# A four-layer graph network on one core: chunks of messages are summed by accumulating transfers before the matrix W2, the last senders of all planes are found in one shared tile, there are fewer columns, and elu is summed on TensorE

## The chip, the cores and the metric

The kernel runs on one core of a Trainium2 chip. The metric is the device time of one execution in microseconds (us), lower is better. Engines are called as in the profile: PE is TensorE (PEld its weight loads), DVE is VectorE, ACT is ScalarE, POOL is GpSimd, SP is SyncE, which only issues transfers here.

## The reference, cut to what matters

There are 64 graphs ("batches") of 256 nodes with 128 features. Every layer adds its result to `x` and begins with a layer norm without weights and a relu, `h`.

```python
# layer 0: multi-head attention (8 heads of 16), masked by adj == 0, weighted by adj, normalised again
x = x + L0(h, adj)
# layer 1: attention from one sender score and one receiver score, masked softmax
x = x + L1(h, adj)
# layer 2: two graph attention (GAT) layers of 4 heads, each followed by elu(o) = max(o,0) + exp(min(o,0)) - 1
x = x + L2(h, adj)
# layer 3: a message for every pair (i, j), weighted by the adjacency
m_j, m_i = h @ W1[:D], h @ W1[D:]
pre = m_j[:, None, :, :] + m_i[:, :, None, :] + b1
msg = gelu(layernorm(pre, g1, be1))
agg = einsum('bijo,bij->bio', msg, adj)
x = x + layernorm(concat([h, agg]) @ W2 + b2, g2, be2)
```

The adjacency is sparse: each pair is an edge with probability of about 1/16 (3.1% made symmetric), and every node has an edge to itself. In layer 3 a message counts only where `adj` is not zero.

## The kernel before, in words

**Streams.** Each batch goes through six stages, each a Python generator that yields after every few instructions: `first` (f: loads, layer 0, the receivers' ranks), `second` (s: layer 1 and the first GAT), `third` (t: the second GAT, `x2`), `lists` (l: which senders each receiver of layer 3 has), `edges` (e: messages and their sums), `fourth` (u: the last norm and the output). In one round the six stages work on six different batches. The string `ORDER` says in which order the generators are advanced within a round: a letter runs its stage to the next yield. `START` gives the round in which a stage begins, and how many of its first letters are passed over, which shifts the stage within the round. Every engine and SP executes its instructions in exactly that order (`tc.manual_schedule()`), and an instruction that waits holds up all behind it on its engine.

**Ranks.** `mha` counts the zeros of each row of the adjacency on PE, and ranks the receivers by their number of senders (L380 to L401). Two indirect transfers on POOL (`in_order`, L695) write the adjacency rows to DRAM in the order of the ranks (`adr_d`), two more write the normalised features (`xn_d`).

**Lists.** `lists` needs three numbers for every edge: the sender's number (`key`), the edge weight and the variance of its message. They are packed into three `planes` of [128, 2, 256], each element carrying the sender's key in its upper bits. MAX8 (L824) finds the eight largest of a row, MATCH_REPLACE8 (L827) takes them out, and so on until `MAXES` = 40 for the block of the 128 highest ranks and 24 for the other are in `best`. The bits are sorted out again (L808 to L851), and the result goes to DRAM as `code_d` (sender numbers, fp16) and `ws_d` (weights and 1/std).

**Edges.** A slot s holds the s-th sender of every receiver. `GROUPS` says how many of the ranked receivers can have a sender in a slot: slots 0 to 15 have all 256 columns, later slots fewer. The groups are laid into five chunks of 1,024 columns: four full ones of four slots, and a last one with the rest. For each chunk `load_chunk` broadcasts code, 1/std and weight to all partitions (`cb`, `rb`, `wb`, L885), with two buffers of each. DVE compares the code with the sender numbers (`chosen`, L903); ACT writes the receivers' part into PSUM (`seeded`, L913); PE adds the senders' part by multiplying with that one-hot matrix (`gather`, L367); DVE multiplies by 1/std (L953), ACT applies gelu (L955), POOL multiplies by the weight (L957). `aggregate` then sums over slots by multiplying each slot with `w2b` on PE into the one tile `agg` (L363); from slot `SUMMED` on, DVE sums the slots of a group first (L929). The chunk before is aggregated while the present one is made.

**elu.** `gat` makes `o` (L661), POOL takes the minimum with 0 (L665), ACT the exponential (L667), POOL max(o, 0) - 1 (L669), and DVE adds the two (L671). The first GAT's result is transposed on PE (L348) and copied by ACT to `g1T`; the second's is added to `xt` (L732).

**Overflow.** Two tests find a receiver with more senders than slots or group hold (L840, L868, L870). If one did, the kernel `every_pair` would run after this one and do all pairs.

Of the kernel before, what the change touches and what calls it, by code (L numbers as in the profile page):

```python
# [8 lines left out]
F32 = mybir.dt.float32  # L9
# [20 lines left out]
SLOTS, MAXES = 36, (40, 24)  # L30
GROUPS = [(0, 4, 256), (4, 4, 256), (8, 4, 256), (12, 4, 256),
          (16, 1, 176), (17, 2, 168), (19, 3, 84), (22, 4, 36), (26, 2, 14), (28, 8, 11)]
SUMMED = 19
# [5 lines left out]
    "fffffstleeeelettfflssfteftesltflseftlfeselfettesetfstststseflfeflletsfetfseeefftfsfllfslffltsessusuf"  # L39
    "uustfffffefffffufutfffletfusfefstetlfsfltltffutettftsulstsfsslefeteleefelflefseetullllslsllesltelllt"  # L40
    "llllllllllelsftsttlfetftllllefsstflusllfltlusfsettffssulleefsefefefeffeetefeleleeeesfefseslslseeeeee"
    "eeelletseelessesfslffselselusslfselffllslstltfleelllfsfllslsllftelsuslfeltslllllefssfllselusseefltss"
    "sesueelleeeeeeelteelsssle"
)

START = {"f": (0, 0), "s": (1, 0), "t": (2, 0), "l": (3, 0), "e": (4, 0), "u": (5, 10)}
# [6 lines left out]
def listed_pairs(  # L53
# [223 lines left out]
    V.tensor_tensor(g1_c, g1_c, down_c, op=ALU.mult)  # L277

# [17 lines left out]
    best = ct([P, 3, NB, MAXES[0]], "best")  # L296
    V.memset(best, 0.0)
    beyond = ct([SLOTS, N], "beyond")
    cap_t, cap_v = ct([SLOTS, 1], "cap_t"), work.tile([1, SLOTS], F32, tag="cap_v", name="cap_v")
    for slot, n, cap in GROUPS:  # L300
        V.memset(cap_v[:, slot:slot + n], cap)
    nc.sync.dma_start(cap_t, cap_v)
    V.tensor_scalar(beyond, nums[:SLOTS, :N], cap_t, None, op0=ALU.is_ge)
    over, over_t = ct([P, 1], "over"), ct([SLOTS, N], "over_t")
    V.memset(over, 0.0)
    V.memset(over_t, 0.0)
# [69 lines left out]
    def mha(hT, ad, adT, xt, rank, adr_d, st):  # L376
# [3 lines left out]
        V.tensor_scalar(mask, ad, 0.0, None, op0=ALU.is_equal)  # L380
# [11 lines left out]
        yield  # L392
        zs = wt([P, N + NB], "zs", st)
# [9 lines left out]
        for nb in range(NB):  # L403
            in_order(adr_d, ad, rank, nb)
            yield
# [93 lines left out]
        for nb in range(NB):  # L499
            V.tensor_tensor(cx[:, nb].rearrange("p (h d) -> p h d", h=HEADS), pn[:, nb, :, 1:1 + HD],  # L500
                            z[:, nb, :, None].to_broadcast([P, HEADS, HD]), op=ALU.mult)
            yield
# [59 lines left out]
    def gat(hT, off, offT, weights, st):  # L562
# [16 lines left out]
        V.tensor_copy(h1, x1)  # L579
# [5 lines left out]
        V.tensor_scalar(ys, x1, rcv, snd, op0=ALU.mult, op1=ALU.add)  # L585
        yield
        V.tensor_scalar(yt[0], x1, snd, rcv, op0=ALU.mult, op1=ALU.add)
# [83 lines left out]
        V.tensor_tensor(o, o, ex, op=ALU.add)  # L671
        yield
        return o


    def several(shape, name, pool=const, dtype=F32, n=2):
# [3 lines left out]
                           several([P, NB, N], "ad"), several([P, NB, N], "adT"))  # L680
# [8 lines left out]
    adr_d, xn_d, ur_d = (several([N, N], "adr_d", dram, n=5), several([N, D], "xn_d", dram, n=3),  # L689
# [7 lines left out]
    def first(b):  # L697

        xt, ad, adT = x1_[b % 3], ad_[b % 2], adT_[b % 2]
# [12 lines left out]
        yield from mha(hT, ad, adT, xt, rank_[b % 6], adr_d[b % 5], "0")  # L712

    def second(b):

        xt, ad, adT = x1_[b % 3], ad_[b % 2], adT_[b % 2]
# [8 lines left out]
        yield from transposed(g1, g1T_[b % 2])  # L725

    def third(b):
# [4 lines left out]
        V.tensor_tensor(x2, xt, g2, op=ALU.add)  # L732
# [8 lines left out]
    def lists(b):  # L741
# [4 lines left out]
        adr, xr, hT = wt([P, NB, N], "adr", "4"), wt([P, NB, D], "xr", "4"), wt([P, N], "hT", "4")  # L746
# [26 lines left out]
        V.tensor_scalar(ciT, p[:, N:], b1_c, down2_c, op0=ALU.add, op1=ALU.mult)  # L773
# [47 lines left out]
        for n in range(3):  # L821
            for nb in range(NB):
                for r in range(0, MAXES[nb], 8):
                    V.max(best[:, n, nb, r:r + 8], planes[n][:, nb])  # L824
                    yield
                    if r + 8 < MAXES[nb]:
                        V.match_replace(planes[n][:, nb], best[:, n, nb, r:r + 8], planes[n][:, nb], 0.0)  # L827
                        yield
# [793 lines left out]
```

## Time and profile before

| | |
|---|---|
| median of 3 runs | 5219.54 us (5213.21 to 5232.44) |
| the profiled execution | 5207.46 us |
| its span | 5205.6 us |
| PE busy | 4491.0 us, 86% |
| DVE busy | 4538.1 us, 87% |
| ACT busy | 3334.4 us, 64% |
| POOL busy | 2672.9 us, 51% |
| DMA, hardware queue | 34.8% of 16 engines, 493.85 MB |
| DMA, software queue (POOL) | 1.9%, 33.58 MB |
| mean granted TensorE clock | 0.957 of full speed |

The span runs from the first to the last instruction; the execution's own time lies 1.9 us over it. In the tables of groups a row gives line, engine, operation, what is written and read, the count, then busy time in all and the mean of one in ns, then the idle time of the engine just before these instructions and who ended it. Busy time counts overlapping instructions once; the mean is of each one's own duration, so that busy over count is below the mean where instructions overlap, as matmuls do. A row of waits gives who waited for whom, the total in us, how often, and the longest.

### The profile page before, as it was taken

Reading aid. Unit: us, or ns where it says so; the run is one execution under the profiler, and the core shown is the slowest. Engines: PE = TensorE matmul, PEld = TensorE weight load, DVE = VectorE, ACT = ScalarE, POOL = GpSimd, SP = SyncE. Lnnn points to the kernel's source line nnn. Section 1 sums busy time; section 2 is a strip of 40 time slices with the busy share of each in tenths; the row PEclk is TensorE's granted clock in tenths of the full one; section 3 lists DMA queues with packets and bytes.
Section 4 is the critical chain, followed back from the end, with each engine's and each line's share of the span. In section 5 each row is a group of like instructions: output and inputs, shape, how many; then the busy total and the mean of one; then the engine's idle time right before and its main releaser. Section 6 shows DMA issues by size and latency. Waiting matters only on the chain. (4 is left out here: it accounts for less than half of the span.)

```text
span 5205.6 us, 89976 instructions
## 1 busy us (share of the span) xinstructions
PE 4491.0 (86%) x30294; PEld 2636.3 (51%) x30294; DVE 4538.1 (87%) x12551; ACT 3334.4 (64%) x6264; POOL 2672.9 (51%) x2890
## 2 busy tenths in 40 slices
PE   5888898888988988988988988988888988998974
PEld 3455555555555555555555555555555555555542
DVE  3688988989988988989988988988988988998985
ACT  2466666666666666667666666666666666666662
POOL 2345555555545545555545545545545545555543
PEclk9899999999999999999999999999999999999997
DMA  1033433333343343343343343343333343343344
GB/s 23 12 113 97 104 116 98 104 117 102 100 118 103 98 118 105 96 118 109 93 118 109 93 118 108 92 118 108 93 118 96 105 117 103 99 118 102 99 117 118
DMA packets 754582, 533.27 MB, mean 102 GB/s; under 512 B 490809, under 2 KB 647614, under 8 KB 754110
## 3 DMA queue, kind: packets, MB, share of 16 engines
q1 hardware_dynamic: 739774, 493.85, 34.8%
q0 software_dynamic: 14336, 33.58, 1.9%
q8 instruction: 241, 3.95, 0.3%
q14 instruction: 231, 1.89, 0.1%
HBM read 479.41 MB, written 47.84 MB: 101 GB/s over the span
## 5 line engine op out<-in xcount | busy, mean ns | idle before, releaser
L957 POOL TENSOR_TENSOR ms<-ms,wb 128x1024 f32<-128x1024 f32 x320 | 754.8, 2359 | 582.9 <-ACT ms L955 476.0
L367 PE MATMUL up<-oh,cj 128*128 128x512 f16 x2560 | 672.1, 400 | 172.0 <-DVE oh L903 96.6
L470 POOL TENSOR_TENSOR ew<-e,adT 128x512 f32<-128x512 f32 x512 | 668.7, 1328 | 62.0 <-ACT e L465 62.0
L363 PE MATMUL agg<-ms,w2b 128*128 128x256 f32 (+2 forms) x2432 | 674.9, 401 | 2.8 <-POOL ms L957 2.8
L824 DVE MAX8 best<-pl 128x8 f32<-128x256 f32 x1536 | 629.1, 420 | 27.0
L330 POOL TENSOR_SCALAR rs<-mv 128x2 f32<-128x2 f32 x256 | 57.5, 225 | 1098.0 <-DVE mv L323 1092.6
L955 ACT ACTIVATE ms<-ms,be,g 128x1024 f32<-128x1024 f32 x320 | 396.7, 1240 | 325.9 <-DVE ms L953 324.5
L629 ACT ACTIVATE ps<-ps 128x512 f32<-128x512 f32 x512 | 277.5, 589 | 414.3 <-PE ps L363 414.2
L367 PEld LDWEIGHTS <-cj 128*128 128x128 f16 x2560 | 251.9, 102 | 494.0 <-issue 162.3
L363 PEld LDWEIGHTS agg<-ms,w2b 128*128 128x128 f32 x2432 | 418.2, 197 | 158.9 <-issue 113.0
L903 DVE TENSOR_SCALAR oh<-cb,code 128x1024 f16<-128x1024 f16 x640 | 344.7, 580 | 163.0 <-DMA cb<-code_d 163.0
L953 DVE TENSOR_TENSOR ms<-up,rb 128x512 f32<-128x512 f32 x640 | 421.1, 682 | 62.9 <-PE up L367 25.8
L827 DVE MATCH_REPLACE8 pl<-best,pl 128x256 f32<-128x256 f32 x1152 | 470.6, 408 | 0.0
L913 ACT ACTIVATE up<-ci 128x512 f32<-128x512 f32 (+6 forms) x896 | 403.0, 477 | 20.7 <-DVE m L605 12.4
L465 ACT ACTIVATE e<-ps 128x512 f32<-128x512 f32 x512 | 276.5, 591 | 173.3 <-PE ps L363 173.3
L444 DVE TENSOR_REDUCE mx_p<-ps 128x2 f32<-128x512 f32 x512 | 332.5, 682 | 19.6 <-PE ps L363 17.4
L605 DVE TENSOR_REDUCE m<-ps 128x2 f32<-128x512 f32 x512 | 331.7, 679 | 6.8 <-PE ps L363 6.8
L638 ACT ACTIVATE y<-ps 128x512 f32<-128x512 f32 x512 | 283.0, 595 | 36.7 <-PE ps L367 33.1
L695 POOL DMA_INDIRECT adr_d<-ad,rank x128 | 134.1, 1048 | 316.8 <-DMA adr_d<-ad,rank 195.6
L340 ACT ACTIVATE xn<-x,nm,rs 128x128 f32<-128x128 f32 x512 | 235.8, 487 | 88.5 <-POOL nm L333 87.8
L363 PE MATMUL ps<-qT,kT 32*128 32x256 f32 x2048 | 291.8, 402 | 0.4 <-DVE qT L451 0.4
L363 PE MATMUL ps<-kT,qT 32*128 32x256 f32 x2048 | 289.9, 400 | 0.0
(295 smaller groups left out, 10615.1 us busy)
## 6 DMA issues: line engine op xcount, KB each, us to landing
rb<-ws_d SPq DMA_DIRECT2D x256, 512.0 KB
wb<-ws_d SPq DMA_DIRECT2D x256, 512.0 KB
cb<-code_d SPq DMA_DIRECT2D x256, 256.0 KB
ad<-in_adj_dram SPq DMA_DIRECT2D x64, 256.0 KB
adr<-adr_d SPq DMA_DIRECT2D x64, 256.0 KB
rb<-ws_d SPq DMA_DIRECT2D x64, 168.0 KB
wb<-ws_d SPq DMA_DIRECT2D x64, 168.0 KB
x<-in_x_dram SPq DMA_DIRECT2D x64, 128.0 KB
```

Of the source, the lines that this page charges most:

```text
L363: return T.matmul(o, lhsT=lhsT, rhs=rhs, start=start, stop=stop)
L367: return T.matmul(o, lhsT=lhsT, rhs=rhs, start=False, stop=False, skip_group_check=True)
L444: V.tensor_reduce(mx_p[:, nb, :, r + j, 0], ps[j], axis=AX.X, op=ALU.max)
L470: G.tensor_tensor(ew[:, r], e[:, r], adT[:, nb:nb + 1, :].to_broadcast([P, HG, N]), op=ALU.mult)
L605: V.tensor_reduce(m[:, k + j], ps[j], axis=AX.X, op=ALU.max)
L824: V.max(best[:, n, nb, r:r + 8], planes[n][:, nb])
L827: V.match_replace(planes[n][:, nb], best[:, n, nb, r:r + 8], planes[n][:, nb], 0.0)
L903: V.tensor_scalar(oh[:, jb], cb, code[:, jb:jb + 1], None, op0=ALU.is_equal)
L913: S.activation(ps[:, lo - h * 512:hi - h * 512].rearrange("p (k n) -> p k n", n=cap), ci_[u][:, None, :cap].to_broadcast([P, (hi - lo) // ...
L953: V.tensor_tensor(ms[:, hs], ps[h], rb[:, hs], op=ALU.mult)
L955: S.activation(ms, ms, AF.Gelu, bias=be1_c, scale=g1_c)
L957: G.tensor_tensor(ms, ms, wb, op=ALU.mult)
```

## The change

- In `edges`, POOL no longer hands every chunk to PE. The first chunk's messages stay in a tile of their own (`whole`), and the next three are added to it by accumulating transfers from POOL's queue. W2 is applied to this sum, four products, and to the last chunk. The step of aggregating the chunk before is gone.
- In `lists`, MAX8 and MATCH_REPLACE8 take 24 and 16 numbers from the rows of the two blocks. What is left of the first 16 rows of one block and the first 26 of the other, of all three planes, goes by six SP transfers into one tile `tail` of 126 rows; up to 16 more are found there, and six transfers bring them back into `best`.
- `GROUPS` has smaller capacities: the last chunk has 898 columns instead of 1,024, and one group more. Slot 19 is no longer summed with others on DVE.
- `gat` returns the two parts of elu. For `g1T` PE multiplies both with the identity and sums them in PSUM; for `x2` POOL adds one part to `xt` and DVE the other.
- Two scalings and a cast in `gat`, and `ciT` in `lists`, go from DVE to ACT. `cx` in `mha` is one operation instead of two.
- The number of zeros of each row goes along as a 257th column of the adjacency (`adz`, `adr_d`), and the overflow test compares its minimum with a table, once at the end.
- `ORDER` and `START` are written anew: 386 letters instead of 425, of them 83 e instead of 96 and 75 l instead of 99.

```diff
-SLOTS, MAXES = 36, (40, 24)
+SLOTS = 36
+MAIN, MORE, TAIL = (24, 16), 16, (16, 26)
 GROUPS = [(0, 4, 256), (4, 4, 256), (8, 4, 256), (12, 4, 256),
-          (16, 1, 176), (17, 2, 168), (19, 3, 84), (22, 4, 36), (26, 2, 14), (28, 8, 11)]
-SUMMED = 19
+          (16, 1, 154), (17, 2, 130), (19, 1, 98), (20, 2, 84), (22, 3, 40), (25, 3, 14), (28, 8, 7)]
+SUMMED = 20
...
-START = {"f": (0, 0), "s": (1, 0), "t": (2, 0), "l": (3, 0), "e": (4, 0), "u": (5, 10)}
+START = {"f": (0, 0), "s": (1, 3), "t": (2, 0), "l": (3, 3), "e": (4, 8), "u": (5, 9)}
...
+        V.tensor_copy(adz[:, :, N], p[:, N:N + NB])
+        yield
...
-        for nb in range(NB):
-            V.tensor_tensor(cx[:, nb].rearrange("p (h d) -> p h d", h=HEADS), pn[:, nb, :, 1:1 + HD],
-                            z[:, nb, :, None].to_broadcast([P, HEADS, HD]), op=ALU.mult)
-            yield
+        V.tensor_tensor(cx.rearrange("p b (h d) -> p b h d", h=HEADS), pn[:, :, :, 1:1 + HD],
+                        z[:, :, :, None].to_broadcast([P, NB, HEADS, HD]), op=ALU.mult)
         yield
...
-        V.tensor_copy(h1, x1)
+        S.activation(h1, x1, AF.Copy)
...
-        V.tensor_scalar(ys, x1, rcv, snd, op0=ALU.mult, op1=ALU.add)
-        yield
-        V.tensor_scalar(yt[0], x1, snd, rcv, op0=ALU.mult, op1=ALU.add)
+        S.activation(ys, x1, AF.Identity, scale=rcv, bias=snd)
+        yield
+        S.activation(yt[0], x1, AF.Identity, scale=snd, bias=rcv)
...
-        V.tensor_tensor(o, o, ex, op=ALU.add)
-        yield
-        return o
+        return o, ex
...
-        yield from transposed(g1, g1T_[b % 2])
+        p = pt()
+        for nb in range(NB):
+            for n in range(2):
+                mm(p[:, nb * P:(nb + 1) * P], g1[n][:, nb, :], ident, start=n == 0, stop=n == 1)
+        yield
+        S.activation(g1T_[b % 2], p[:, :N], AF.Copy)
+        yield
...
-        V.tensor_tensor(x2, xt, g2, op=ALU.add)
+        G.tensor_tensor(x2, xt, g2[0], op=ALU.add)
+        yield
+        V.tensor_tensor(x2, x2, g2[1], op=ALU.add)
...
-        V.tensor_scalar(ciT, p[:, N:], b1_c, down2_c, op0=ALU.add, op1=ALU.mult)
+        S.activation(ciT, p[:, N:], AF.Identity, scale=down2_c, bias=b1d_c)
...
+        V.tensor_tensor(fewest, fewest, adr[:, :, N], op=ALU.min)
+        adr = adr[:, :, :N]
...
+        tail, tops8 = wt([3 * sum(TAIL), N], "tail", "4"), wt([3 * sum(TAIL), MORE], "tops8", "4")
+        def part_of(n, nb):
+            at = n * sum(TAIL) + sum(TAIL[:nb])
+            return slice(at, at + TAIL[nb])
         for n in range(3):
             for nb in range(NB):
-                for r in range(0, MAXES[nb], 8):
+                for r in range(0, MAIN[nb], 8):
                     V.max(best[:, n, nb, r:r + 8], planes[n][:, nb])
                     yield
-                    if r + 8 < MAXES[nb]:
-                        V.match_replace(planes[n][:, nb], best[:, n, nb, r:r + 8], planes[n][:, nb], 0.0)
-                        yield
+                    V.match_replace(planes[n][:, nb], best[:, n, nb, r:r + 8], planes[n][:, nb], 0.0)
                     yield
+                nc.sync.dma_start(tail[part_of(n, nb)], planes[n][:TAIL[nb], nb])
+                yield
+        for r in range(0, MORE, 8):
+            V.max(tops8[:, r:r + 8], tail)
+            yield
+            if r + 8 < MORE:
+                V.match_replace(tail, tops8[:, r:r + 8], tail, 0.0)
+                yield
+        for n in range(3):
+            for nb in range(NB):
+                nc.sync.dma_start(best[:TAIL[nb], n, nb, MAIN[nb]:MAIN[nb] + MORE], tops8[part_of(n, nb)])
+                yield
...
-        V.tensor_tensor(over, over, best[:, 0, 0, SLOTS:SLOTS + 1], op=ALU.max)
-        yield
...
-        G.tensor_tensor(far, rows_t[:SLOTS], beyond, op=ALU.mult)
-        yield
-        G.tensor_tensor(over_t, over_t, far, op=ALU.add)
         yield
...
-            ms = edge.tile([P, COLS], F32, tag="ms", name="ms", bufs=3)
+            w = widths[c]
+            halves = [slice(0, 512), slice(512, w)]
+            ms = edge.tile([P, COLS], F32, tag="ms" if c else "whole", name="ms", bufs=3 if c else 1)
...
-            G.tensor_tensor(ms, ms, wb, op=ALU.mult)
+            G.tensor_tensor(ms[:, :w], ms[:, :w], wb[:, :w], op=ALU.mult)
             yield
+            if c == 0:
+                whole = ms
+            elif c < CHUNKS - 1:
+                G.dma_start(whole, ms, accum_op=ALU.add)
+                yield
...
             yield
-            if before is not None:
-                yield from aggregate(c - 1, before)
-            before = ms
+        yield from aggregate(0, whole)
         yield
-        yield from aggregate(CHUNKS - 1, before)
+        yield from aggregate(CHUNKS - 1, ms)
```

## The prediction

> **What bounds the kernel now.** I read the page's busy shares first, then a stretch of ten batches in the middle, then DVE's waits there, then the groups that the change touches.
>
> ```profile
> PE 4491.0 (86%) x30294; PEld 2636.3 (51%) x30294; DVE 4538.1 (87%) x12551; ACT 3334.4 (64%) x6264; POOL 2672.9 (51%) x2890
> L859 DVE CAST code<-pt x64: 415/417/418, 274.7 to 5136.8; 36x256 f16<-36x256 f32 x64
> 2000.00:2771.80 771.80, 685.50 (x4715) 404.31 (x4714) 701.80 (x1935) 519.58 (x972) 416.01 (x445) 0.98 0.39 106
> DVE oh L903 <- DMA cb<-code_d: 104.0, 41, 3.7
> DVE o L671 <- POOL o L669: 61.7, 40, 1.6
> DVE code L859 <- PE pt L855: 12.4, 40, 0.3
> ```
>
> Line 2 is an operation that runs once a batch: its first and last start give a **period** of (5136.8 - 274.7)/63 = 77.2 us, and a fixed part of 5205.6 - 63 x 77.2 = 343 us. Line 3 (columns: window, its length, busy of PE, PEld, DVE, ACT, POOL, clock, DMA share, GB/s) covers ten periods. Per period DVE is busy 70 us (69.7 over the 40 periods from 1046.5), PE 68.5, ACT 52, POOL 41.6. Two engines are at 90%, each in a hand-written order. DVE's idle 7.5 us is in the last three lines (40 periods): 2.6 us for the first chunk's code columns, 1.5 us for POOL inside elu, 0.3 us; the rest is gaps too small for the view. The page's chain of waits names only the tail of the run, each share 0%, and carries nothing. So a microsecond counts if it leaves both DVE and PE, or if it is a wait on their queues.
>
> ```profile
> L824 DVE MAX8 best<-pl 128x8 f32<-128x256 f32 x1536 | 629.1, 420 | 27.0
> L827 DVE MATCH_REPLACE8 pl<-best,pl 128x256 f32<-128x256 f32 x1152 | 470.6, 408 | 0.0
> L827 DVE MATCH_VALUE_LOAD pl<-best,pl 128x8 f32 x1152 | 103.7, 90 | 28.9
> L671 DVE TENSOR_TENSOR o<-o,ex 128x256 f32<-128x256 f32 x128 | 86.5, 676 | 101.6 <-POOL o L669 101.6
> L363 PE MATMUL agg<-ms,w2b 128*128 128x256 f32 x2048 | 606.8, 417 | 0.0
> L957 POOL TENSOR_TENSOR ms<-ms,wb 128x1024 f32<-128x1024 f32 x320 | 754.8, 2359 | 582.9 <-ACT ms L955 476.0
> POOL adr_d L695 <- DMA adr_d<-ad,rank: 195.6, 63, 4.3
> 2618.00:2620.00 2.00, 2.00 (x12) 1.16 (x11) 1.93 (x6) 1.04 (x4) 0.00 (x0) 1.00 1.06 420
> ```
>
> The matmul row is 32 records a batch for 16 full-width products with W2: each fp32 product is two records. They overlap, so its price is busy over count, 606.8/2048 = 0.296 us, not the mean 417 ns. The last line is DMA at its fullest: 420 GB/s.
>
> **What the Trainium skill says.** (1) "DMA: Bandwidth & Descriptors", section "Anatomy of one DMA — SWDGE (gpsimd) path": a transfer takes about 2.0 us plus bytes over 436 GB/s, most of the fixed part being the receipt. This trace agrees: 420 GB/s above, and POOL's indirect transfers land 2.2 to 2.4 us after issue. (2) "Collectives: The Full Stack", section "The bandwidth ceiling: the fold count and why AG ≠ RS ≠ AR": a reducing transfer is slow because it reads two sources, not because of the add. No run here shows one yet. (3) The first page, "Rules for kernel authors": an accumulate must wait for the earlier accumulate of the same bytes; the built order of the changed kernel has those waits on POOL. (4) "SBUF — State Buffer", section "Who interferes with whom": a DVE operation with two SBUF inputs and a POOL operation that reads SBUF block each other. The trace agrees: L671 takes 409 ns at best, 676 on average.
>
> **The change part by part, per batch.** From the two built orders, counts are exact.
>
> *Lists, DVE.* MAX8 24 to 15, MATCH_REPLACE8 18 to 15; on the shared tail two and one are added. -9 x 0.410 - 3 x (0.409 + 0.090) + 2 x 0.410 + 0.499 = **-3.9**. The overflow test (L840, 0.15) becomes a minimum of two columns (0.15) and a copy of two counts from PSUM (about 0.2, nearest the reciprocal of 128x8 from PSUM, 0.2): +0.2.
>
> *elu and gat, DVE.* Both o + ex go (L671): -2 x 0.676; third() keeps one add, with ex in place of o. The cast of h1 (0.286), ys (0.407) and yt (0.405) move to ACT, twice a batch: -2.2. ciT moves too (-0.54); cx is one operation for two (-0.14). Together **-4.2**. The last chunk is 898 columns for 1024: two comparisons (0.54 each), one product (0.66) and four sums shrink, **-0.4**. DVE in all -8.3: 69.7 becomes **61.4**.
>
> *PE.* Four full chunks are summed to one before W2: 12 of 16 products go, -24 x 0.296 = **-7.1**. g1T: two transposes (0.25 each) become four matmuls of 128x128 with the identity, eight records at the price of pt<-gs,lo (72.8/512 = 0.142): +0.6. Narrower gathers -4 x 0.2625 x 0.25 = -0.26; slot 19 gets its own product, +0.2. PE -6.5: 68.4 becomes **61.9**.
>
> *ACT* gains 2 x 0.38 + 4 x 0.59 + 0.47 + 0.2 for one more seeding, **+3.8**, to 55.5. Table loads stay eight a round. It is hidden as long as ACT, at 79% of the new period, is not late for PE.
>
> *POOL.* far and over_t go (-1.5), xt + o comes (+0.74), the last product is narrower (-0.3), and three accumulates are issued. An issue isn't in the trace; nearest is DMA_INDIRECT, 1.05 us; below, it can't be under zero; above I allow 2.5. 3 x 1.05: **+2.1** in all, to 43.1, with idle time to hide in.
>
> *The accumulates' landing* (T). Plain, 0.52 MB costs 2.0 + 1.2 = 3.2 us by the skill's formula; with two reads 2.0 + 2.5 = **4.5**, my estimate; at the mean 107 GB/s of the middle stretch two reads take 10, my upper end. Order on POOL: product 1, accumulate 1, both adr_d writes, product 2, accumulate 2 (waits for 1), both uu gathers, product 3, accumulate 3 (waits for 2). Cover of the first wait is two issues, the 3.1 us between them (195.6/64) and a product: 2.1 + 3.1 + 2.36 = 7.5 us. Cover of the second is 2.1 + 2.36 = 4.5. PE's first product with the sum stands behind the last chunk's gather, mask and score matmuls of mha and a whole y product, over 8 us later. At 4.5 us all is covered. DMA work grows from 0.39 x 77.2 = 30 us by 3 x 2.5, to half of the period.
>
> *SP.* Twelve tail transfers and three more chunk pieces are issued, 0.44 us each (median of the cb issues): 6.6 us, in front of the next x, ad, code_d and chunk loads. *New DVE waits:* the tail's last transfer needs 0.44 + 2.3, and DVE has four reductions, three small operations and ym in front of the MAX8 on tail, 2.6 + 0.5 + 0.4 = 3.5 us: covered. (2.3: code_d is issued at 2608.47 and the cb load that needs it at 2610.76.) Going back, six issues in a row: the first pair lands 0.9 + 2.3 after the last MAX8, DVE has 1.9 us in between (an add, four statistics, cn): 1.3 us idle; the second reader needs the sixth, 2.6 + 2.3: another 1.3. Behind it wait reciprocal, code16 and so the next loads. **+2.6**, bounds 0 and 4.9. ym after mrows has lost the MAX8 that stood in between: +0.5. POOL's wait in elu (1.5) leaves DVE. Code columns: x and ad are now ahead of code_d, which could take 2.6 off; g1T's longer way (POOL, ACT, PE) could put as much back: 0 taken, both ends kept.
>
> *Sum.* DVE 61.4 + 7.5 - 1.5 + 2.6 + 0.5 = 70.5; PE 61.9 + its idle 8.8 = 70.7. Period **70.6**. Of the fixed 343 us some 45 is setup (first POOL transfer waits at 49.6); the rest scales: 45 + 298 x 70.6/77.2 = 318. Span 63 x 70.6 + 318 = 4766, against 5205.6; execution 1.9 us more, 4768 against 5207.46. The median of the runs, 5219.54, stands 0.23% above the profiled one: **4779**, rounded to 4775.
>
> **Rivals.** *A, round trips uncovered.* If SP is late by its queue (its waits are in order, and a tail transfer stands behind out and ur), both trips are bare: 2.8 + 4.9 for 2.6, period 75.7, 5110. For: SP already waits 1505 us on others at L864. Against: the fillers on DVE.
>
> *B, the sum waits on PE.* The W2 products filled PE while DVE worked; without them PE idles and the DVE-PE exchanges set the pace, say 3 us more: 73.6, 4980. For: both engines idle on each other now. Against: those waits are under 2 us each.
>
> *C, slower: the accumulates are late.* Each T beyond the covers blocks POOL, (T - 7.5) + (T - 4.5), and behind it the next statistics, the last product and ew for mha. POOL has about 9 us of slack there (up to 11.9 before L330). The lost time passes the gain of 6.6 us from T of about 14; at 16 us it is 11 over: period 81.6, 5520. For: no such transfer in this trace. Against: 14 is three times my estimate.
>
> *D, it falls back.* If a receiver had more senders than the tighter groups hold, every_pair would run as well, and the time would rise by thousands. I counted the reference's adjacency: at most 34 senders against 40 found, and no batch breaks the new capacities.
>
> **How the numbers follow.** A measurement of this kernel can tell about 0.5% from no change. As planned 0.72 (4570 to 4900: period 67.5 to 72.5), A 0.11, B 0.08, C 0.08, D 0.01. The range runs from 4560 to 5040, the whole of the planned case and B and the near part of A. Faster by over 0.5%: 0.72 + 0.08 + 0.08 of A = 0.88; same 0.03; slower 0.09.
>
> **What would show it.** Right: period near 70.6 by the same L859 row; DVE near 61.4 and PE near 62 per period; 8 full-width W2 records a batch; accumulates landing in 4 to 6 us; DVE idle 1 to 3 us a batch before the first reader of best, none before the MAX8 on tail. Wrong: POOL waiting on accumulates (C), DVE waiting on tail (A), or the period above 77.

## The result, and the profile after

The changed kernel is **slower**: 5451.77 us median of 4 runs (5407.54 to 5465.76) beside 5223.18 us for the kernel before (4 runs), ratio 1.042 with a 95% interval of 1.036 to 1.049. The forecast was 4775 us. The profiled execution took 5461.06 us.

Three lines of the page and of two views answer those shown of before: the busy times, the operation that runs once a batch (now L885), and the window of 40 batches.

```profile
PE 4465.1 (82%) x29205; PEld 2471.4 (45%) x29270; DVE 4020.1 (74%) x11275; ACT 3526.0 (65%) x6777; POOL 2770.6 (51%) x3018
L885 DVE CAST code<-pt x64: 406/409/417, 273.0 to 5379.6; 36x256 f16<-36x256 f32 x64
1083.60:4326.00 3242.40, 2730.35 (x18061) 1515.04 (x18098) 2477.76 (x6897) 2193.49 (x4208) 1710.00 (x1856) 0.91 0.48 121
```

The kernel before had this in its own 40 batches:

```profile
1046.50:4133.70 3087.20, 2736.47 (x18697) 1612.84 (x18695) 2788.64 (x7675) 2067.81 (x3879) 1649.01 (x1780) 0.97 0.39 107
```

The period is (5379.6 - 273.0)/63 = 81.06 us, for 77.2 before and 70.6 forecast. The third line of the first fence, divided by its 40 periods, gives the surprise: DVE is busy 61.9 us a batch (forecast 61.4), ACT 54.8 (55.5), POOL 42.8 (43.1). **The work fell as forecast, and the period rose.** DVE is now idle for 81.06 - 61.94 = 19.1 us a batch where it was 7.5. Only PE's 68.3 is off (61.9 forecast), and there the granted clock stands beside it: 0.91, where the kernel before had 0.97.

So the question is what the engines wait for. The waits in the same 40 batches (who waits for whom, us in all, times, longest):

```profile
DVE x L582 <- ACT wa L580: 279.4, 75, 6.2
DVE cn L493 <- PE pt L368: 146.2, 38, 5.1
PE pt L353 <- ACT xn L345: 120.6, 106, 6.0
ACT up L935 <- DVE mx_p L451: 184.3, 39, 9.6
ACT xn L345 <- POOL nm L338: 121.9, 96, 5.5
POOL uu L1015 <- DMA ur_d<-ur: 328.4, 38, 9.9
```

DVE waits 7.0 us a batch for ACT at the first operation on `x1` in `gat` (L582) and 3.7 for PE at `cn`, the weighted sums of layer 0's attention; no engine is full. Read upwards from the last line they look like one chain: POOL stands 8.2 us a batch at the first `uu` gather, then makes `nm` late, ACT's `xn` is late, PE's transposes (L353) are late. One batch shows why POOL waits; first SP's queue (start, length, what, how many):

```profile
2737.94 5.81 SPq L907 DMA_DIRECT2D cb<-code_d  x7
2743.84 5.29 SPq L907 DMA_DIRECT2D rb<-ws_d  x7
2750.62 5.01 SPq L907 DMA_DIRECT2D wb<-ws_d  x7
2755.73 1.51 SPq L1036 DMA_DIRECT2D out_dram<-un  x1
2757.41 0.36 SPq L1012 DMA_DIRECT2D ur_d<-ur  x1
```

ACT had made `ur` at 2744.46, but its transfer stands behind 21 pieces of the last chunk, and they take (5.81 + 5.29 + 5.01)/21 = 0.77 us each; my price was 0.44. The pieces are not slow by themselves. Six of them took 3.02 us in the kernel before, 0.50 each, and seven took 3.37 to 4.17 us, 0.53 each, in `no_accum` below, the changed kernel without its accumulates:

```profile
2644.87 3.02 SPq L885 DMA_DIRECT2D cb<-code_d  x6
```

```profile
2760.51 4.17 SPq L907 DMA_DIRECT2D cb<-code_d  x7
2764.77 3.67 SPq L907 DMA_DIRECT2D rb<-ws_d  x7
2773.82 3.37 SPq L907 DMA_DIRECT2D wb<-ws_d  x7
```

In 40 batches of the changed kernel a piece that SP began to issue 2 to 3 us after an accumulate took 1.42 us on average (70 of them), one begun less than 1 us after it 0.48 (117; the first piece of a row, which can wait for its buffer, is not counted). In the batch above the first `wb` piece also had to wait until POOL's second product was done, at 2750.59.

POOL in the same batch, with the idle time ahead in brackets:

```profile
2750.89 0.96 POOL L987 DMA_DIRECT2D ms<-ms  x1 [0.30 <-POOL ms L982]
2760.17 1.06 POOL L1015 DMA_INDIRECT uu<-ur_d,rank  x1 [8.31 <-DMA ur_d<-ur]
2762.50 2.41 POOL L982 TENSOR_TENSOR ms<-ms,wb 128x1024 f32<-128x1024 f32 x1
2765.21 0.99 POOL L987 DMA_DIRECT2D ms<-ms  x1 [0.30 <-POOL ms L982]
2767.71 0.20 POOL L338 TENSOR_TENSOR nm<-nm,rs 128x2 f32<-128x2 f32 x1
```

The third product, its accumulate (0.99 us to issue) and the scalars of a norm follow the gathers. And PE, which needs that norm, with the windows around it:

```profile
2764.68 1.05 PE L368 MATMUL pt<-y,ones 128*32 128x256 f32 x16
2768.49 0.47 PE L353 MATMUL pt<-ident,xn 128*128 128x128 f32 x1 [2.76 <-ACT xn L345]
2770.32 1.12 PE L659 MATMUL pt<-ident,nd 128*128 128x128 f32 x4 [0.50 <-ACT nd L654]
```

```profile
2764.00:2766.00 2.00, 1.73 (x32) 0.78 (x24) 1.86 (x7) 1.66 (x3) 1.70 (x2) 1.00 0.05 13
2766.00:2768.50 2.50, 0.01 (x1) 0.01 (x1) 2.36 (x9) 0.56 (x2) 2.11 (x6) 0.90 0.81 154
2768.50:2772.50 4.00, 3.11 (x10) 2.35 (x11) 2.32 (x8) 2.05 (x5) 4.00 (x4) 0.50 0.24 46
2772.50:2776.00 3.50, 3.50 (x32) 2.19 (x34) 2.05 (x10) 1.07 (x3) 2.48 (x3) 0.67 0.00 0
```

The clock is the third number from the end: after 2.76 us of idleness PE runs at 0.50, until the window with 0.67. The granted clock is either 1.00 or 0.50 in both traces, so that a mean of 0.91 means half speed for 2 x 0.09 x 81 = 14.6 us of each batch; 0.97 meant 2 x 0.03 x 77.2 = 4.6. The Trainium skill, "TensorE: Matmul & The Clock Gate", section "Part 1: The HAM clock gate", says this: PE is halved after an idle window of about 3.4 us and freed after one that is busy. The trace agrees in kind, but a gap of 2.76 us was enough: by the windows the clock fell some 2.3 us into it (0.5 of the 2.5 us up to 2768.50 are at half speed), and it stayed down for 0.5 + 4.0 + 2.3 = 6.8 us.

### The profile page after: what moved, and what is told of

Same layout as the page of the kernel before. It is cut to its first block, busy times and chain, and to the rows that moved or that the text cites. A ratio compares the mean times of both kernels' runs of the same rounds, so it can differ in the third digit from the quotient of the medians.

```text
span 5459.3 us, 89242 instructions
## 1 busy us (share of the span) xinstructions
PE 4465.1 (82%) x29205; PEld 2471.4 (45%) x29270; DVE 4020.1 (74%) x11275; ACT 3526.0 (65%) x6777; POOL 2770.6 (51%) x3018
## 3 DMA queue, kind: packets, MB, share of 16 engines
q0 software_dynamic: 41984, 134.32, 11.4%
## 5 line engine op out<-in xcount | busy, mean ns | idle before, releaser
L982 POOL TENSOR_TENSOR ms<-ms,wb 128x1024 f32<-128x1024 f32 (+1 forms) x320 | 743.2, 2323 | 691.4 <-ACT ms L980 666.4
L372 PE MATMUL up<-oh,cj 128*128 128x512 f16 (+1 forms) x2560 | 708.8, 413 | 195.5 <-ACT up L937 133.7
L978 DVE TENSOR_TENSOR ms<-up,rb 128x512 f32<-128x512 f32 (+1 forms) x640 | 430.6, 674 | 163.9 <-PE up L372 81.0
L980 ACT ACTIVATE ms<-ms,be,g 128x1024 f32<-128x1024 f32 (+1 forms) x320 | 390.3, 1220 | 238.3 <-DVE ms L978 232.9
L1015 POOL DMA_INDIRECT uu<-ur_d,rank x128 | 130.8, 1022 | 595.9 <-DMA ur_d<-ur 517.9
L842 DVE MAX8 best<-pl 128x8 f32<-128x256 f32 x960 | 406.9, 424 | 20.0
L582 DVE SCALAR_TENSOR_TENSOR x<-h,lane,pt 128x256 f32<-128x256 bf16 x128 | 61.3, 479 | 454.0 <-ACT wa L580 454.0
L844 DVE MATCH_REPLACE8 pl<-best,pl 128x256 f32<-128x256 f32 x960 | 392.2, 409 | 0.0
L451 DVE TENSOR_REDUCE mx_p<-ps 128x2 f32<-128x512 f32 x512 | 329.1, 686 | 79.2 <-PE ps L368 77.5
L937 ACT ACTIVATE up<-ci 128x512 f32<-128x512 f32 (+5 forms) x832 | 375.3, 466 | 8.1
L610 DVE TENSOR_REDUCE m<-ps 128x2 f32<-128x512 f32 x512 | 328.4, 683 | 64.6 <-PE ps L368 58.9
L925 DVE TENSOR_SCALAR oh<-cb,code 128x1024 f16<-128x1024 f16 (+1 forms) x640 | 325.6, 551 | 18.6 <-DMA cb<-code_d 18.3
L368 PE MATMUL agg<-ms,w2b 128*128 128x256 f32 (+3 forms) x1024 | 296.4, 401 | 41.5 <-DMA ms<-ms 41.5
```

What stands on the lines that cost most here:

```text
L368: return T.matmul(o, lhsT=lhsT, rhs=rhs, start=start, stop=stop)
L372: return T.matmul(o, lhsT=lhsT, rhs=rhs, start=False, stop=False, skip_group_check=True)
L451: V.tensor_reduce(mx_p[:, nb, :, r + j, 0], ps[j], axis=AX.X, op=ALU.max)
L610: V.tensor_reduce(m[:, k + j], ps[j], axis=AX.X, op=ALU.max)
L925: V.tensor_scalar(oh[:, jb, :w], cb[:, :w], code[:, jb:jb + 1], None, op0=ALU.is_equal)
L937: S.activation(ps[:, lo - h * 512:hi - h * 512].rearrange("p (k n) -> p k n", n=cap), ci_[u][:, None, :cap].to_broadcast([P, (hi - lo) // ...
```

## Experiments

Theories at the start: **1**, SP's queue (the late `ur_d` holds POOL and the chain behind it); **2**, the accumulates' load on the DMA engines; **3**, the new order with chains that run over several engines; later **4**, PE's clock. The "middle period" of the expectations is the mean of batches 20 to 59, 78.1 us before and 81.7 after, somewhat above the period from first to last start that the table gives. Each ratio is to the kernel before on the same chip; a point is 0.01 of it.

| run | ratio (95%) | period | clock |
|---|---|---|---|
| before | | 77.2 | 0.957 |
| after | 1.042 (1.036 to 1.049) | 81.1 | 0.895 |
| ur_act | 1.098 (1.093 to 1.103) | 85.8 | 0.857 |
| no_accum | 1.044 (1.037 to 1.051) | 81.9 | 0.881 |
| all_old_order | 1.069 (1.066 to 1.072) | 83.3 | 0.902 |
| part_accum | 1.049 (1.046 to 1.052) | 81.7 | 0.903 |
| accum_filled | 1.055 (1.051 to 1.059) | 82.1 | 0.929 |
| accum_late | 1.031 (1.028 to 1.035) | 80.1 | 0.901 |
| accum_late2 | 1.022 (1.018 to 1.027) | 79.4 | 0.906 |
| part_tail | 1.031 (1.028 to 1.035) | 80.2 | 0.935 |
| part_elu | 0.997 (0.995 to 0.999) | 77.3 | 0.965 |
| part_elu_dve | 1.007 (1.005 to 1.009) | 78.2 | 0.959 |
| after_filled | 1.016 (1.013 to 1.020) | 78.9 | 0.937 |
| undo_accum | 1.057 (1.050 to 1.065) | 82.8 | 0.909 |
| undo_ur_elu | 1.077 (1.073 to 1.082) | 83.8 | 0.917 |
| ur_first | 1.026 (1.020 to 1.032) | 79.9 | 0.894 |
| ur_first_filled | 1.012 (1.010 to 1.014) | 78.7 | 0.927 |
| ur_fill_elu | 0.997 (0.996 to 0.998) | 77.6 | 0.940 |
| ur_fill_elu2 | **0.982** (0.979 to 0.985) | 76.1 | 0.942 |
| ur_elu2 | 1.016 (1.013 to 1.019) | 78.8 | 0.905 |

### The transfer of ur, on ACT's queue and earlier on SP's

`ur_act`:

```diff
-        nc.sync.dma_start(ur_d[b % 2].rearrange("(a p) d -> p a d", p=P), ur)
+        nc.scalar.dma_start(ur_d[b % 2].rearrange("(a p) d -> p a d", p=P), ur)
```

> The changed kernel with one edit: the transfer of ur to DRAM (ur_d, which both uu gathers on POOL read) is issued from ACT's queue right behind the copy that makes ur, and not from SP. Theory 1 (SP's queue): in the changed kernel ur_d is issued some 13 us after ur is ready, because 21 pieces of the last chunk and the output stand in front of it, and POOL waits for uu 8.3 us a batch (517.9 us in the run), which holds up the third product, its accumulate, the statistics' scalars and the last product. Then POOL's wait for ur_d falls below 3 us a batch, and the period from 81.1 to about 76: about 5135 us. Theory 2 (load of the accumulating transfers) and theory 3 (the new order with its chains POOL, ACT, PE, DVE): the wait at uu falls as well, but the time stays within 1% of 5452, since another wait takes its place.

Slower by 5.6 points, which no theory had. Waits in the same window as above:

```profile
POOL uu L1015 <- DMA ur_d<-ur: 48.9, 30, 2.7
ACT ps L634 <- DMA rb<-ws_d: 158.5, 37, 6.1
```

POOL's wait is gone (48.9 us for 328.4), but ACT now stands 4.3 us a batch at the place of the issue: by the trace it is released by the landing of an earlier transfer of SP's queue (`rb`), and all of ACT stands behind it. Batch for batch, DVE is 6.9 us later than in the changed kernel ahead of the gathers (L451) and 4.3 behind them (L582). The second step is what an early `ur_d` gives, 2.6 us; the first is a new wait.

`ur_first` moves 14 pieces instead. `pieces` issues what the loop did; `edges` calls the last chunk's `weights` after the seeds of the fourth, which is behind `ur_d` in SP's order:

```diff
-        for t, src, row in ((cb, code_d[u], 0), (rb, ws_d[u], SLOTS), (wb, ws_d[u], 0)):
...
+        def weights():
+            pieces((rb, ws_d[u], SLOTS), (wb, ws_d[u], 0))
+        pieces((cb, code_d[u], 0))
+        if c < CHUNKS - 1:
+            weights()
+        return cb, wb, rb, weights
...
+            if c == CHUNKS - 2:
+                loads[c + 1][3]()
```

> The changed kernel with one edit in SP's order: the 14 rb and wb pieces of the last chunk are issued behind the transfer of ur instead of ahead of it (the 7 cb pieces stay ahead). No other engine's order changes. Theory 1 (ur_d late in SP's queue holds POOL at the uu gathers, and behind it the norm's scalars, ACT's xn and PE): POOL's wait for ur_d falls from 8.2 us a batch to below 2, the middle period from 81.7 to 79 (the run with ur_d on ACT won back 2.6 us behind the gathers while it lost 6.9 ahead of them), about 5270 us, ratio to before 1.00 to 1.015. Rival (the wait is hidden anyway, clock and chains set the time): within 0.7% of 5452 us.

1.026: 1.6 points won, 1.2 us of the period. POOL waits for `ur_d` only twice in the whole run, and `ur_d` is issued 0.6 us after `ur` is made, for 12.4 in the changed kernel and 0.2 in the kernel before (medians of 40 batches). Theory 1 is right in kind and four tenths of the loss in size, less than expected: the gathers moved 8.7 us ahead, `nm` 4.9, DVE's L582 1.6.

### The accumulates' load

`no_accum`:

```diff
-                G.dma_start(whole, ms, accum_op=ALU.add)
```

> The changed kernel without its three accumulating transfers: the messages of chunks 1 to 3 are left out of the sum, all else is issued as before. Theory 2 (their load on the DMA engines makes SP's pieces slow to issue and other transfers late): pieces issue at 0.55 us again, and the period falls from 81.1 to 75 or below, 5070 us. Theory 1 (SP's queue behind the pieces): only POOL's three issues go (3 x 0.99 us), POOL still waits 6 us or more a batch for ur_d, and the period falls by 1 to 3 us, 5260 to 5390 us. Theory 3 (the order): a fall of at most 1 us, 5390 us or above.

1.044, no gain within the interval, though the software queue's share falls from 11.4% to 1.8%. One half of theory 2 came true: without the accumulates SP's pieces are issued at 0.53 us again, and `ur_d` 9.3 us after `ur` instead of 12.4. But POOL still waits 318.7 us for it in the 40 batches (328.4 with them), and the time stays. So the accumulates do slow SP, but in the new order they are not what sets the period, and POOL's three issues (3 us) were not on the path either.

### The parts alone, in the order of the kernel before

`all_old_order` keeps `ORDER` and `START` of before and puts bare yields where steps went.

> The changed kernel's instructions in the order of the kernel before: its order string and start table, with empty steps where the change removed one (each accumulate behind its product, the four products with the sum where the fourth chunk was aggregated). Theory 3 (the loss comes from the newly written order): the period is 72 to 74, about 4900 us, since DVE's 8 us and PE's 6.5 us of removed work come through. Theory 1: in this order ur_d stands elsewhere in SP's queue, so the period also falls, but the 12 tail transfers and three more pieces still cost SP some 10 us, period 76 to 79, 5130 to 5330 us. Theory 2 (load of the accumulates, whatever the order): 80 or above, 5400 us.

1.069, in the range that theory 2 had named. The newly written order isn't the loss; it takes 2.6 points of it back. That leaves the parts; the three that were run alone cost 4.9, 3.1 and -0.3 points, 7.7 for these 6.9. The smaller groups and the new overflow test were not run alone.

`part_accum`:

```diff
-            if before is not None:
-                yield from aggregate(c - 1, before)
+            if c == 0:
+                whole = ms
+            elif c < CHUNKS - 1:
+                G.dma_start(whole, ms, accum_op=ALU.add)
...
+            if c == CHUNKS - 1:
+                yield from aggregate(0, whole)
+            elif c:
+                for _ in range(6):
+                    yield
```

> The kernel before, in its own order, with one part of the change: chunks 0 to 3 are summed by three accumulating transfers and W2 is applied to the sum, in the place where the fourth chunk was aggregated. PE loses 12 of 16 products, 7.1 us of 68.4 a batch; DVE's 69.7 us stay. Theory 1 and theory 3 (the accumulates are harmless by themselves): DVE bounds it, period 75.5 to 77, ratio to before 0.98 to 1.00, and PE's own busy time falls to 61 or 62. Theory 2 (load): slower than before, period 79 or above, ratio 1.02 or more, with longer landings of the chunk pieces.

1.049 with an unchanged order, above the 1.02 of theory 2: 7.1 us of PE's work less by the count of products, 4.5 us of period more. PE's busy time fell by only (4491.0 - 4324.4)/64 = 2.6 us a batch, at a clock of 0.903 for 0.957. SP's small pieces are not slower here (0.50 us on average, as in the kernel before), so this is not the load that theory 2 meant. PE waits for the third landing, `PE agg <- DMA ms<-ms`, 154.4 us in 64 times; a landing takes 4.6 to 7.7 us, median 6.3, in the 27 of 192 for which the trace has it.

`accum_filled` puts twelve products with a zero tile in place of those removed (main line of the edit against `part_accum`).

```diff
+                    mm(agg, wz, ones, start=False, stop=False)
```

> The kernel before with the accumulating transfers (as in the run of that part alone), and in the places of the 12 products with W2 that went, 12 products of the same size with a tile of zeros as weights and a tile of ones as data, added into agg: no work of the reference, nothing to wait for, only PE kept as busy as before. New theory 4 (the clock): without those products PE stands idle for 2 to 4 us several times a batch and then runs at a clock of 0.50 for some 4 us; filled, the granted clock is back at 0.95 or more, PE's gaps before the gathers go, and the period falls from 81.6 to 77 to 78, ratio to before 0.99 to 1.01, although 7.1 us of work were added to the part alone. Rival (the accumulates cost by themselves: POOL's issues, the DMA load, PE's wait for the last landing): ratio stays at 1.04 or above, since more work on PE can only add.

The clock rose from 0.903 to 0.929 and the time did not fall, 1.055. In this order theory 4 does not explain the loss. `accum_late` moves the sum's four products to the end of the stage (main lines of the edit against `part_accum`).

```diff
-                yield from aggregate(0, whole)
...
         yield from aggregate(CHUNKS - 1, ms)
+        for _ in aggregate(0, whole):
+            pass
```

> The kernel before with the accumulates alone, and the four products with the sum moved behind the last chunk's, to the end of the stage (about 8 us later on PE). In the run with the accumulates alone PE waited 2.3 us a batch for the third landing, and all behind it ran 2.2 us later. Theory (exposed landing): that wait goes, middle period from 82.6 to 80 to 80.5, about 5350 us; the rest of the loss stays, as the DVE operation on x1 of gat that takes 2.97 us on average for 1.58 before. Rival (clock or load): no gain, 5480 us or more.

1.031: the exposed landing was 1.8 points. `accum_late2` also moves the second accumulate's issue on POOL past the third `ew` (edit against `accum_late`).

```diff
-            elif c < CHUNKS - 1:
+            elif c in (1, 3):
                 G.dma_start(whole, ms, accum_op=ALU.add)
+            prev = ms
...
+                if c == 3 and h == 0:
+                    G.dma_start(whole, prev, accum_op=ALU.add)
```

> As accum_late (the kernel before with the accumulates, the sum's products at the end), but the second accumulate is issued after the third ew product of mha instead of between ex and o of elu. In accum_late that issue pushes o and the two ew products on POOL 0.3 us later, so that ew starts ahead of DVE's operation on x1 of gat (L581) and not behind it; L581 then takes 2.97 us on average for 1.58, and ACT's yt, the next seeds and PE's gather run 1.8 us later. Theory[...]: L581 is back at 1.6 us or less, middle period from 81.1 to 79.3, about 5290 us. Rival (the clock: the gather after it runs at half speed for want of the products): period within 0.5 of 81.1, 5370 us or more.

1.022, 0.9 points more. The reason is to be seen on two engines in the timeline. `part_accum`:

```profile
2061.34 0.95 POOL L961 DMA_DIRECT2D ms<-ms  x1
2062.07 1.47 POOL L669 TENSOR_SCALAR o<-o 128x256 f32<-128x256 f32 x1
...
2063.28 2.70 POOL L470 TENSOR_TENSOR ew<-e,adT 128x512 f32<-128x512 f32 x2
2063.33 2.94 DVE L581 SCALAR_TENSOR_TENSOR x<-h,lane,x 128x256 f32<-128x256 bf16 x1
```

and `accum_late2`:

```profile
2020.21 1.58 DVE L581 SCALAR_TENSOR_TENSOR x<-h,lane,x 128x256 f32<-128x256 bf16 x1
2020.24 2.67 POOL L470 TENSOR_TENSOR ew<-e,adT 128x512 f32<-128x512 f32 x2 [0.72 <-ACT e L465]
```

L581, with two SBUF inputs, takes 0.48 us undisturbed. Where POOL starts 0.05 us ahead, DVE is held for both `ew`, 2.94 us; where DVE starts 0.03 us ahead, about for one, 1.58. The Trainium skill, "SBUF — State Buffer", section "Who interferes with whom", says that issue order decides who blocks; here too, though going first did not free DVE altogether. One 0.95 us issue had turned the order round, and ACT's `yt` waited 160.9 us for L581 in the whole run of `part_accum`, 72.4 in that of `accum_late2`. The last 2.2 points of `part_accum` I did not find.

`part_tail`, the shared search alone:

> The kernel before, in its own order, with one part: the shared tail search (24 and 16 numbers from the planes, six transfers into one tile, 16 more found there, six transfers back). DVE loses 3.9 us of 69.7; PE is untouched. As predicted: round trip 2.6 us on DVE, period 77.2 to about 76, ratio 0.98 to 0.99. Theory 1 (SP): 12 more issues at 0.5 to 0.8 us and both trips bare, 7.7 us idle on DVE for 3.9 gained: ratio 1.02 to 1.05. Theory 4: no more PE gaps than before if DVE is not late, clock 0.95 or more.

1.031, between 1.02 and 1.05 as theory 1 said. Its waits in the whole run:

```profile
DVE part L809 <- DMA best<-tops: 321.2, 128, 4.1
DVE tops L839 <- DMA tail<-pl: 76.9, 47, 3.5
```

The way back costs DVE 5.0 us a batch, the way there 1.2, for 3.9 us of work. In the new order the same two waits are 13.9 and 4.4 us in the whole run: there the order covers them.

`part_elu`, elu and the moves from DVE to ACT alone:

> The kernel before, in its own order, with one part: elu's two parts summed on PE for g1T and on POOL and DVE for x2, and the casts and scalings h1, ys, yt and ciT on ACT. DVE loses 4 us a batch, ACT gains 3.6, PE 0.6. As predicted: DVE bounds, period 77.2 to 73.5 to 75, ratio 0.95 to 0.98. Theory 3 (the chain from POOL over ACT to PE grows longer and DVE only waits elsewhere): ratio 0.99 to 1.03, with DVE waiting on ACT for ys, yt and the products made of them.

0.997, theory 3. DVE's busy time fell by 4538.1 - 4271.6 = 267 us, 4.2 a batch as forecast, and came back as waits (whole run; the first was 163.0 us before, the others below 18):

```profile
DVE oh L912 <- DMA cb<-code_d: 262.1, 71, 5.7
DVE m L607 <- PE ps L365: 113.7, 68, 2.7
DVE bs L324 <- DMA x<-in_x_dram: 65.0, 60, 2.3
```

`part_elu_dve` adds minimum and maximum of elu on DVE.

> The kernel before with the part elu and ACT moves, and besides the minimum and the maximum of elu on DVE instead of POOL: 1.4 us more on DVE (which had lost 4.2), a shorter chain ahead of g1T. In part_elu the freed 4 us of DVE came to nothing (ratio 0.997). Theory 3 (chains between engines set the period, not DVE's sum): ratio 0.985 to 0.995. Rival (DVE's sum counts): 1.4 us a batch slower than part_elu, ratio 1.01 to 1.015.

1.007, a point slower: here neither theory is clean, since 1.4 us of work cost 0.9 us.

### PE's clock in the new order

`after_filled` adds twelve zero products a batch to the changed kernel, ahead of what PE waits for: two ahead of each norm's transposes, one ahead of the matmuls of `g1T`, one ahead of each chunk's gather.

```diff
+        for _ in range(fill):
+            mm(p[:, :N], wz, ones)
...
+        mm(p[:, :N], wz, ones)
...
+            mm(agg, wz, ones, start=False, stop=False)
```

> The changed kernel with 12 such zero products a batch ahead of instructions that PE waits for: two before the transposes after each of three norms, one before each chunk's gather, one before the four matmuls of g1T. No work of the reference is left out. Theory 4 (the clock): granted clock from 0.895 to 0.94 or more, period from 81.1 to 77 or below, below 5200 us. Theory 1 (POOL's wait for uu behind SP's pieces sets the period): the wait stays at 8 us a batch and the time stays at 5400 to 5500 us. Theory 3 (PE and DVE chains of the new order): 7 us more on PE make it slower, 5500 us or more.

1.016: 7 us of PE work that computes nothing made a batch 81.06 - 78.91 = 2.15 us shorter, about half of what theory 4 had said, while POOL still waits 8 us for `ur_d`. `undo_accum` puts the real products back instead, four at a time one step after each product.

```diff
-                G.dma_start(whole, ms, accum_op=ALU.add)
+                for _ in aggregate(c - 1, before):
+                    pass
```

> The changed kernel with one part undone: no accumulating transfers; in their places (one step after each product) PE multiplies the chunk before with W2, as in the kernel before, and the fourth chunk where the sum was multiplied. POOL loses three issues of 0.99 us a batch, PE gets 7.1 us of real work that waits for nothing. Theory 4 (clock): these products keep PE warm as the zero products did, granted clock 0.93 or more, middle period from 81.7 to 79.5 or below, about 5320 us. Theory 1: the late ur_d and its wait of 8 us a batch stay. Rival (W2 products are work that the accumulates really save): the time stays at 5430 us or above.

1.057, slower than the change. My expectation fails: PE's clock hardly rose (0.909 for 0.895), and DVE's `mx_p` (L451) comes 2.9 us later; each burst of some 2.0 us stands ahead of the scores that DVE waits for. The twelve zero products, which won, had been put where PE waits anyway. `undo_ur_elu`, with the two edits of the next part, fails the same way:

> As undo_accum, with the rb and wb pieces of the last chunk behind ur_d on SP and elu's minimum and maximum on DVE. If the three losses are separate: middle period 77 or below (the filled version with the same two edits has 78.0, and POOL's three issues go here), 5130 to 5200 us, ratio to before 0.98 to 0.995. If the zero products stood in better places than the real ones: 5230 us or more.

1.077. How the products of W2 fare in better places was not tried.

### Both, and elu's chain

> The same order on SP, and the 12 zero products a batch on PE of the filled version of the changed kernel. If the late ur_d and the clock are two separate losses, their gains add: 79.4 less 2.6, middle period 76.8, about 5150 us, ratio to before 0.985. If the fills only paid for PE's gap that the late ur_d makes, the result is that of one of them alone, 5250 to 5320 us.

1.012: together 3.0 points for 1.6 and 2.6 alone, so they overlap, and one reason can be seen: PE's wait for `xn` at L353 fell from 120.6 to 43.8 us in `ur_first` already, and two of the zero products stand in the same gap.

`ur_fill_elu` also takes elu's two halves from POOL to DVE, `ur_fill_elu2` makes the second right behind the first, as in this diff, instead of after the exponential:

```diff
-        G.tensor_scalar(ex, o, 0.0, None, op0=ALU.min)
+        V.tensor_scalar(ex, o, 0.0, None, op0=ALU.min)
+        V.tensor_scalar(o, o, 0.0, 1.0, op0=ALU.max, op1=ALU.subtract)
         yield
         S.activation(ex, ex, AF.Exp)
         yield
-        G.tensor_scalar(o, o, 0.0, 1.0, op0=ALU.max, op1=ALU.subtract)
```

> As the version before, and the minimum and the maximum of elu (ex, o) are done by DVE and not by POOL. DVE stands idle there (4.6 us ahead of the second residual of gat in the filled version, 1.0 us ahead of zg) since it waits for the chain POOL, ACT, PE, ACT that these two begin; POOL's two take 0.86 and 1.08 us, on DVE about 0.3 to 0.4 each. Theory 3 (chain): 0.6 to 1.2 us a batch faster than without, about 5090 us. Rival (DVE's busy time counts): 4 x 0.35 us slower, 1.4 us a batch, 5240 us.

> As ur_fill_elu, with one DVE instruction a layer moved: o = max(o, 0) - 1 right behind ex = min(o, 0), instead of a step after ACT's exponential. If the chain o (DVE), x + o and the last four ew (POOL), ew products (PE), cn (DVE) sets the end of the batch, POOL starts ew some 4 us earlier, DVE's 4.0 us ahead of cn shrink to below 1, and the middle period falls from 78.0 to 75 to 76.5, about 5060 us, ratio to before 0.96 to 0.975. Rival (another chain ends at the same time): 77.3 or more, ratio 0.985 or above.

0.997 and **0.982**: 1.5 points each, and the second is a version that beats both kernels, 5132.84 us median of 4. The first is 1.1 us a batch faster than `ur_first_filled`, as theory 3 said; its absolute forecasts had started from a time that `ur_first_filled` did not reach. The same move cost a point in the old order (`part_elu_dve`), so its worth depends on the order around it. The second falls short of its expectation: DVE still waits 3.2 us a batch at `cn` (138.0 us in 43), where less than 1 was expected, so that chain has another link which I did not follow.

`ur_elu2` is the same without the zero products:

> The same without the zero products on PE. If the clock is a loss of its own (theory 4), it is slower than the version with them by 1.5 to 2.3 us a batch, about 5180 us, with a granted clock near 0.90. If the shorter chains have closed PE's gaps, both are within 0.5%.

1.016, so the zero products alone are worth 3.3 points here. The windows of `ur_elu2` and then of `ur_fill_elu2`, PE busy first, the clock third from the end:

```profile
1083.60:4326.00 3242.40, 2796.18 (x18708) 1531.14 (x18748) 2627.65 (x7302) 2265.97 (x4353) 1617.59 (x1764) 0.92 0.49 125
```

```profile
1083.60:4326.00 3242.40, 2959.14 (x20292) 1701.99 (x20331) 2620.01 (x7523) 2332.94 (x4473) 1659.32 (x1818) 0.95 0.49 128
```

## Why the prediction was wrong

- **The step that failed** is the sum, "DVE 61.4 + 7.5 - 1.5 + 2.6 + 0.5" and "PE 61.9 + its idle 8.8". It carried the old idle times over as constants. DVE's idle became 19.1 us. Neither engine had bounded the kernel by its work: `part_elu` took 4.2 us from DVE and 0.3% from the time, `part_accum` took twelve products from PE and lengthened it. What counted here were the waits between the engines, and the sum let none of them grow except by the 3.1 us for `best` and `ym`.
- **SP** was the mis-sized term. 0.44 us, the median of the `cb` issues, was near the 0.50 of a piece in the kernel before. But the accumulates lengthen the issues that follow them, so that with their waits for buffers rows of seven take 0.77 us each, and the prediction had a term for the accumulates' landing and none for this. The larger part is the place of `ur_d` in the queue: it is issued 12.4 us after `ur`, still 9.3 without the accumulates, and 0.2 in the kernel before. Rival A named "a tail transfer stands behind out and ur" and took the wrong victim: `ur_d` itself stood behind the pieces, and POOL behind `ur_d`. The trips of `tail` and `best` were covered (0.3 us a batch, 2.6 forecast).
- **PE's clock** had no term, though the kernel before showed it at 0.98 in ten batches and 0.97 in forty. Forecast 61.9 us busy, measured 68.3 with eight W2 records a batch, as counted (512 in the run); such a record now takes 520 ns on average for 417. Rival B, "without them PE idles", was the nearest, but put it at 3 us; the idleness also halved the clock of the work behind it, as the windows above show.
- **elu**: "POOL's wait in elu (1.5) leaves DVE" was right as to that wait, and DVE's work fell as forecast, but other waits took its place (`part_elu`, 0.997). `ex` and `o` had stood on POOL before the change as well. With the other two edits in place, giving them to DVE won 3.0 points.
- **The accumulates**: T measured 6.3 us (4.6 to 7.7, in `part_accum`) and 6.5 (4.6 to 9.1, in the new order of `ur_first`, all 192) for my 4.5; no run shows whether the two reads are the reason. The covers held in the new order: POOL waited 10.0 us for an earlier landing in the whole run, PE 41.5 us in 3 times. Rival C is out. Its list of what stands behind POOL was right, for another cause.
- **Right**: DVE's, ACT's and POOL's work within 1.5%; that `every_pair` does not run (D); the code columns' wait went (L925 waits for `cb` 18.3 us in all, 163.0 before for L903).
- **Slips** that decide nothing: POOL's sum is 1649.01/40 + 2.1 = 43.3, not 43.1; two reads of 1.2 us are 2.4, not 2.5; rival A's period gives 5120 us, not 5110; and the 2.2 to 2.4 us of POOL's indirect transfers are their minimum and median, the longest of those took 5.2.

What is settled: the edits to `ur_d`, to PE's gaps and to elu together made the difference between 1.042 and 0.982. Of the three only the late `ur_d` is shown to have come with the change (0.2 us became 12.4). PE's lower clock came with it too, but whether zero products would also speed up the kernel before was not run. Still open is the way from there to the forecast: 76.1 us a batch for 70.6, with DVE idle for 14.6 us, 8 of them at the first operation on `x1` in `gat` and at `cn`.

## What to carry to other kernels

Where two engines are nearly full and wait for each other, do not simply subtract removed work from the period; take it away in a run, or follow one batch's chain first. Whenever a step is given to a queue (SP, POOL), list what is queued behind it and who waits for that, and take the issue times from a stretch in which the same other transfers are under way. When work leaves PE, look at what its gaps do to the clock; work that computes nothing, placed where PE waits anyway, can pay. It won 2.4% and 3.3% in the new order and nothing in `accum_filled`, so it has to be run.

## What was not expected of the hardware

- Zero products that add 0.6 us each to PE made the kernel 2.4% and, in another version, 3.3% faster (5451.77 to 5319.98, 5305.54 to 5132.84 us).
- A start 0.05 us earlier on POOL made a DVE operation take 2.94 us instead of 1.58, against 0.48 undisturbed.
- In `ur_act` ACT, which issued one transfer, stood still for 3.4 us in one batch until an earlier transfer of SP's queue had landed.
- An accumulating transfer of POOL's slowed the issues on SP's queue: a broadcast piece begun 2 to 3 us after it took 1.42 us on average, against 0.48 for one begun less than 1 us after it and 0.48 on average in the run without accumulates (`no_accum`).
